# A convolution-and-attention kernel whose image seams are rebuilt: the next image's first convolution piece inside the last attention unit, spread statistics, and pools on exchanged sides

## The chip, the cores and the metric

The kernel runs on one core of one Trainium2 chip. The metric is the device time of one execution in microseconds (us), lower is better. All data are 32-bit floats, and the on-chip memory (SBUF) has 128 partitions, one per channel or token of a tile.

The engines are TensorE (PE, matmuls; PEld is its weight load), VectorE (DVE), ScalarE (ACT), GpSimd (POOL) and SyncE (SP). ACT, POOL and SP also issue transfers (DMAs), each from a queue of its own that is worked off in order.

## The reference, cut to what matters

The input holds 4 images of 128 channels and 64 x 64 positions (4096 tokens). Each image goes through three layers; what comes out has the input's shape.

```python
# layer 0: 1x1 convolutions of the group-normalised image, attention over all 4096 positions
x = x + _L0_conv_ref(_gn(x), w1, b1, a1, w2, b2, a2, wa, ba, aa)
#   e1, e2 = prelu(w1 x + b1), prelu(w2 x + b2)      (64 rows each)
#   out = softmax(e1^T e2) . prelu(wa x + ba)^T
# layer 1: "quantum ring" attention with 16 heads of 8, then a small feed-forward network
t = _to_tokens(x)
t = t + _L1_attn_ref(_ln_t(t), rx_theta, ry_theta, w_comb, ...)
#   q = ring(cos(heads + rx)); scores = q q^T / sqrt(8); ctx = softmax(scores) q
# layer 2: a linear map, normalised over all tokens of all images, and a recurrent scan
t = t + _L1_ffn_ref(_ln_t(t), W, V, gamma, beta)
x = _from_tokens(t, x)
```

The group norm `_gn` needs the mean and variance of every 4 channels over the whole image before the first convolution can begin.

## The kernel before, in words

The main loop handles the images one after another. For each one, `first_stage` (pools named `conv{n}`) does layer 0, and `second_stage` (pools named `attn{n}`) the 16-head attention of layer 1. The feed-forward network of image n is worked off in small steps between the matmuls of image n+1's first stage; that of image 3 has a `last_stage` of its own. Then comes the scan over all images.

**First stage.** `layer0` begins with `first_pieces`: two 512-column pieces of the image are normalised (L393), multiplied by the joined weights for queries and keys (`conv_matmuls`, L406), passed through two relus (L413, L414) and joined (`conv_joins`, L425 to L430) into `e12` and `e2`. The values come from `third_matmuls` (a bias matmul at L274, four at L442) and a prelu (L352 to L354). `halves` splits the first 512 queries into a high and a low part (L499, L500), two copies on ACT (L480) put them on the other 64 partitions, and then the softmax attention over 8 query groups `ic` and 16 key pairs `jp` can begin: scores (L518), exponentials (L522), weighing (L529). The other convolution pieces (`both_convs`, `third_conv`) are done between the first steps of that loop. `take` copies each result (`taken`, in the `half` pool), and `tokens` turns it to token order: `px` and `pt` are transposes on PE (L269), `sum` (L640) adds up the softmax sums held in `total` (pool `sums`). Its last parts write the layer 1 queries into `parts_dram`, from where the second stage reads them.

**Second stage.** `attention` runs over 8 head pairs and 4 query blocks each. A block has 20 units (blocks 0 and 1) or 16 units (blocks 2 and 3). Each unit has four score matmuls (L1072), the exponentials (ACT, L1084), transposes of them (VectorE, L847), mirrored products (PE, L860; added up by VectorE, L874) and weighing (PE, L881). `finish` ends a block: VectorE transposes the result into `o` (L919, a tile of the pool `half`, which has one buffer here), and POOL copies it out in 16 small copies (L927). `prepare` loads the queries (L777) and the keys (L786) of a pair from `parts_dram` through SP; of the four key blocks, block 1 is loaded first. Both pools have six buffers. While an image's attention goes on, its input `xs` is no longer wanted, and the function `exps` uses that memory as further buffers.

**The next image.** `prepare_image` is a generator that the attention calls in its last block: at unit 0 it loads the next image into `xs` (L142), and in the last eleven units it does the eight `bn_stats` (L365), the aggregate (L368), and the two small matmuls over the groups of four channels (L372, L381), with `rsqrt` (L217 on VectorE, L219 on POOL). For image 0 the same function runs before `layer0`, and between its steps the generator `first_weights` changes signs of `aa` and `a12` (L297, L298) and splits a bias row (L302, L303). The first eight weight loads come through ACT's queue (L150, L163, L173).

**Order and memory.** The order of PE, ACT and VectorE (in the attention of POOL too) is the one written in the code; SP's queue is put in order by the framework's scheduler. A stage's pools are stacked from the left or the right end of SBUF, in the order in which `stage` opens them. A buffer of a new pool may lie on memory of a closed one: its first writer waits until the old tile's last reader is done. Image n's `q` (16 KB per partition) lies at the left end for even and at the right end for odd n. Before, all pools of a first stage lie on the left (default), as do those of a second stage, but for the keys, which for even images lie on the right. Sizes per partition: a `HALF` tile has 2 KB, `MID` 4 KB, `BIG` 16 KB, a key tile 4 KB, a query tile 2 KB.

Of the kernel before, what the change touches and what calls it, by code (L numbers as in the profile page):

```python
# [26 lines left out]
def kernel(  # L27
# [31 lines left out]
    nc = tc.nc  # L59
# [28 lines left out]
    def stage(name, sides={}, others={}, **pools):  # L88
# [3 lines left out]
        with ExitStack() as stack:  # L92
            for kind, (shape, bufs) in pools.items():
                space = PSUM if kind.startswith("ps_") else bass.MemoryType.SB
                pool = stack.enter_context(
# [4 lines left out]
                        side=sides.get(kind),  # L100
# [4 lines left out]
            here.update(others)  # L105
            yield
# [39 lines left out]
    loader = [nc.scalar]  # L146
# [25 lines left out]
    for i, ap in enumerate((a1, a2)):  # L172
        nc.scalar.dma_start(out=a12_sb[ts(i, CR), :], in_=ap.partition_broadcast(CR))  # L173
# [187 lines left out]
    def norm_stats(n, xs):  # L361

        st = once.tile([P, NIC, 6], F32, tag="gst", name=f"gst{n}")
        for i in range(NIC):
            nc.vector.bn_stats(st[:, i, :], xs[:, ts(i, IC)])  # L365
            yield
# [5 lines left out]
        nc.tensor.matmul(pg[:, 0:1], grp, mv[:, 0:1], **alone)  # L372
        gm = once.tile([P, 1], F32, tag="gm", name=f"gm{n}")
# [7 lines left out]
        nc.tensor.matmul(pv[:, 0:1], grp, tv, **alone)  # L381
        yield gm, rsqrt(pv[:, 0:1], 1e-5, [P, 1], f"g{n}")

    def layer0(n, xs, xh, norm, shifted, begin, meanwhile):
# [13 lines left out]
        asmT = big_tile(f"asmT{n}")  # L398

# [17 lines left out]
        def conv_joins(i, j0, j1, y, z):  # L417

            cols = slice((2 * i + j0) * IC, (2 * i + j1) * IC)

            def parted(ap):
                return ap.rearrange("p (a b) -> p a b", b=IC)

            joined = parted(e12[:, cols])
            nc.vector.scalar_tensor_tensor(  # L425
                joined, z[:, j0:j1], a12_sb, y[:, j0:j1], ALU.mult, ALU.add
            )
            high, low = parted(e2[CR:P, cols]), parted(e2[0:CR, cols])
            nc.vector.tensor_copy(high.bitcast(F32R), joined[CR:P])
            nc.vector.tensor_tensor(low.bitcast(F32R), joined[CR:P], high, ALU.subtract)  # L430
# [7 lines left out]
        def third_matmuls(i, j, to):  # L438

            bias_first(to, 0)  # L440
            for k in range(TG):
                nc.tensor.matmul(  # L442
                    to[:, ts(k, P)],
                    xh[:, ts(TG * (2 * i + j) + k, P)],
                    wa_sb,
                    start=False,
                    stop=True,
                    skip_group_check=True,
                )

        def third_conv(i):
# [4 lines left out]
            to = pair(asmT[:, ts(i, 2 * IC)])  # L456
# [5 lines left out]
        def first_pieces():  # L462

            normalised(0, 1)
            pc = pair_psum(f"pc{n}_0")
            conv_matmuls(0, (0,), pc)
            normalised(1, 2)
            conv_matmuls(0, (1,), pc)
            early = conv_relus(0, 0, 1, pc)
            pas = [one_psum(f"pa{n}_0_{j}") for j in range(2)]  # L470
            for j in range(2):
                third_matmuls(0, j, pas[j])
            conv_joins(0, 0, 1, *early)
            if not shifted:
                halves(0)
            late = conv_relus(0, 1, 2, pc)
            if not shifted:
                for y in range(2):
                    hl = state["halves", 0][:, y, :].bitcast(F32R)
                    nc.scalar.copy(hl[CR:P], hl[0:CR])  # L480

            def join_third(j):
                ya, za = half_tile(f"ya{n}_0_{j}"), half_tile(f"za{n}_0_{j}")
                prelu(asmT[:, ts(j, IC)], pas[j], ya, za, (0.0, 0.0), aa_sb)
# [1554 lines left out]
```

## Time and profile before

| what | value |
|---|---|
| time, median of 3 runs | 6962.41 us (6960.99 to 6967.05) |
| the profiled execution's own time | 6967.16 us |
| its span in the profile | 6965.4 us |
| mean clock granted to TensorE | 0.988 |
| ACT L1084, exponentials of the 16 heads, two targets | 2953.1 + 1840.6 us |
| VectorE L847, their transposes, two sources | 2594.3 + 1562.5 us |
| PE L860 / L881 / L1072, second stage | 1969.8 / 1525.6 + 942.3 / 1245.7 us |
| PE L529 / L518, first stage | 947.1 / 588.6 us |
| ACT L522, exponentials of the first stage | 500.1 us |
| POOL L927, copies of `o` | 430.4 us |

The groups in the page's list give a line of the code, an engine, an operation, the tiles written and read, and the total busy time. The profile covers one execution; its span begins a little after the start of the time that is measured and ends a little before its end. Durations of single instructions are taken from this execution. DMAs of 256 KB each make up the keys (256 of them) and, among others, the loads of the images from `x`; the queries are 1024 DMAs of 32 KB, all from SP's queue. SP stands waiting for L1072 before its L786 loads for 1425.7 us in 105 cases (the longest 29.0 us), and before its L777 loads for 1696.0 us in 52 cases (the longest 38.2 us).

### The profile page before, as it was taken

How to read it: one execution, taken by the hardware profiler on the slowest of the kernel's cores; microseconds unless marked ns; L12 is line 12 of the kernel's file. 1: busy time of each engine (PE TensorE's matmuls, PEld its weight loads, DVE VectorE, ACT ScalarE, POOL GpSimd, SP SyncE). 2: the span in 40 equal slices, each digit the busy share in tenths (PEclk: the TensorE clock that was granted, in tenths of full speed). 3: DMA queues.
4: the chain of work that ended last, by engine and by line, in shares of the span. 5: the costliest groups of instructions: out<-in, count | busy, mean ns of one | idle time of the engine just before them, and what ended most of it. 6: DMA issues, size and time to landing. Idle time of an engine off the chain costs nothing. (4 is left out here: it accounts for less than half of the span.)

```text
span 6965.4 us, 223500 instructions
## 1 busy us (share of the span) xinstructions
PE 6819.4 (98%) x92343; PEld 3661.7 (53%) x92343; DVE 5971.6 (86%) x8073; ACT 5936.1 (85%) x11841; POOL 2789.8 (40%) x10000
## 2 busy tenths in 40 slices
PE   9999999999999999999999999999999999999997
PEld 5545555555664555555565455555456555555555
DVE  6688889887888898888787889898978898889888
ACT  4479999996669999999665999999956699999985
POOL 0134444434333444443433344344343343444443
PEclk9999999999999999999999999999999999999998
DMA  1110000000111000000011100000001100000012
GB/s 32 40 37 25 25 27 21 22 10 23 46 52 42 28 21 22 21 22 9 31 49 52 37 22 21 21 21 24 22 22 50 50 33 21 22 24 24 20 62 110
DMA packets 85975, 219.86 MB, mean 32 GB/s; under 512 B 10008, under 2 KB 11040, under 8 KB 84176
## 3 DMA queue, kind: packets, MB, share of 16 engines
q1 hardware_dynamic: 82316, 200.09, 8.5%
q8 instruction: 726, 11.89, 0.7%
q10 hardware_dynamic: 2628, 5.38, 0.2%
q14 instruction: 305, 2.50, 0.1%
HBM read 141.44 MB, written 56.62 MB: 28 GB/s over the span
## 5 line engine op out<-in xcount | busy, mean ns | idle before, releaser
L1084 ACT ACTIVATE e<-s 128x1024 f32<-128x1024 f32 (+1 forms) x3480 | 2953.1, 903 | 115.4 <-PE s L1072 84.6
L847 DVE STREAM_TRANSPOSE t<-e 128x1024 f32<-128x1024 f32 x2240 | 2594.3, 1210 | 78.0 <-ACT e L1084 75.3
L860 PEld LDWEIGHTS misc<-t,mirror 128*32 128x32 f32 x57344 | 1657.0, 110 | 1327.2 <-issue 1272.7
L860 PE MATMUL misc<-t,mirror 128*32 128x128 f32 x57344 | 1969.8, 273 | 16.8 <-DVE later L874 14.0
L1084 ACT ACTIVATE xs<-s 128x1024 f32<-128x1024 f32 (+1 forms) x2152 | 1840.6, 909 | 52.7 <-PE s L1072 40.8
L847 DVE STREAM_TRANSPOSE t<-xs 128x1024 f32<-128x1024 f32 x1344 | 1562.5, 1210 | 42.7 <-ACT xs L1084 41.3
L881 PE MATMUL acc<-e,q_aug 128*32 128x512 f32 x11360 | 1525.6, 609 | 0.0
L1072 PE MATMUL s<-queries,keys 32*128 32x512 f32 x9216 | 1245.7, 497 | 20.7 <-ACT e L1084 9.3
L927 POOL COPY own<-o 32x36 f32<-32x36 f32 x2048 | 430.4, 210 | 1803.1 <-DVE o L919 1723.2
L529 PE MATMUL acc<-p,asmT 128*128 128x512 f32 x2048 | 947.1, 594 | 0.4 <-ACT p L522 0.4
L881 PE MATMUL acc<-xs,q_aug 128*32 128x512 f32 x7072 | 942.3, 605 | 0.0
L522 ACT ACTIVATE p<-s 128x1024 f32<-128x1024 f32 x512 | 500.1, 1023 | 402.9 <-PE s L518 398.9
L1072 PEld LDWEIGHTS s<-queries,keys 32*128 32x128 f32 x9216 | 488.1, 182 | 602.3 <-issue 299.8
L952 POOL COPY other<-turned 32x64 f32<-32x64 f32 x1904 | 451.9, 237 | 622.5 <-DVE turned L942 544.0
L1084 ACT ACTIVATION_READ_ACCUMULATOR e<-s 128x1 f32 x2880 | 695.6, 242 | 0.0
L817 POOL COPY mirror<-q 32x128 f32<-32x128 f32 x2048 | 604.1, 295 | 198.6 <-PE misc L860 110.7
L518 PE MATMUL s<-hl,e 128*128 128x512 f32 x2048 | 588.6, 428 | 22.7 <-ACT hl L480 11.3
L543 DVE TENSOR_TENSOR total<-total,p 128x1024 f32<-128x1024 f32 x448 | 547.7, 1223 | 24.7 <-ACT p L522 17.3
L529 PEld LDWEIGHTS acc<-p,asmT 128*128 128x128 f32 x2048 | 380.1, 190 | 334.0 <-issue 310.4
L518 PEld LDWEIGHTS s<-hl,e 128*128 128x128 f32 x2048 | 380.7, 189 | 180.2 <-issue 69.2
L1084 ACT ACTIVATION_READ_ACCUMULATOR xs<-s 128x1 f32 x1728 | 421.7, 244 | 0.0
L913 POOL COPY by_token<-by_key 32x4 f32<-32x4 f32 x2000 | 385.5, 193 | 84.5
(320 smaller groups left out, 4440.3 us busy)
## 6 DMA issues: line engine op xcount, KB each, us to landing
keys<-parts_dram SPq DMA_DIRECT2D x256, 256.0 KB
queries<-parts_dram SPq DMA_DIRECT2D x1024, 32.0 KB
x_dram<-x SPq DMA_DIRECT2D x56, 256.0 KB
fx<-x_dram SPq DMA_DIRECT2D x48, 256.0 KB
t_dram<-t2T SPq DMA_DIRECT2D x32, 256.0 KB
t2s<-t_dram SPq DMA_DIRECT2D x16, 512.0 KB
hl<-hl SPq DMA_DIRECT2D x28, 256.0 KB
parts_dram<-high SPq DMA_DIRECT2D x28, 256.0 KB
```

The costliest lines, as they stand in the source:

```text
L518: nc.tensor.matmul(s[:, j, :], stationary, moving, start=y == 0, stop=y == len(parts) - 1)
L522: nc.scalar.activation(p, s, AF.Exp)
L529: nc.tensor.matmul(state["acc", ic], asmT[:, ts(2 * jp + j, P)], p[:, j, :], start=jp == 0 and j == 0, stop=jp == NP - 1 and j == 1,)
L543: nc.vector.tensor_tensor(state[ic], state[ic], p, ALU.add)
L817: nc.gpsimd.tensor_copy(wv[ts(a, 32), s, :, :, ts(a, D)], own[ts(s, 32)])
L847: nc.vector.transpose(group["e"][h][:, k, :], es[h])
L860: nc.tensor.matmul(state["acc"][ts(2 * x + h, 32), :], state["w"][:, QT * (s // 4) + TG * x + s % 4, h, :], state["e"][h][:, :, ds(IC * x ...
L881: nc.tensor.matmul(it["in"]["acc"][ts(2 * h + x, 32), :], it["qa"][:, ds((2 * it["tiles"][x] + h) * V, 32)], it["e"][h][:, ts(x, IC)], sta ...
L927: nc.gpsimd.tensor_copy(own[ts(s, 32), ts(x, 4), h, :], ov[ts(2 * h + x, 32), s, :, 0:V])
L952: copy(to[ts(k, 32), h], tv[ts(2 * x + h, 32), k])
L1072: nc.tensor.matmul(ss[h][:, x, :], keys[unit[x] // QT].bitcast(F32R)[r, ts(unit[x] % QT, P)], queries[b].bitcast(F32R)[r, :], start=True, ...
L1084: nc.scalar.activation(es[h][:, ts(x, IC)] if split else es[h], ss[h][:, x, :] if split else ss[h].rearrange("p x c -> p (x c)"), AF.Exp, ...
```

## The change

The change has five parts.

1. **The first piece.** `first_pieces` is gone. A new generator `opening` does the first 512 columns only (normalise, the joined and the value convolution, joins, split, copies). For images 1 to 3 it is stepped by the attention in the last unit of its last block: a step after the exponentials, a step after the weighing, a step at the end of the unit, and the rest behind the loop. The second piece (`second_piece`) comes after the first scores of `layer0`, and the other normalises are spread over the loop.
2. **Where it lies.** `stage` can close some pools early. The attention's `queries` and `keys` are closed in the last unit, and `place_of_first` puts the query halves `hl` and three tiles (the first 512 columns of keys, values and joined) into their memory; `rooms`, a pool for scratch, follows. `e12`, `e2` and `asmT` of `layer0` are 512 columns shorter, and `beyond` picks the tile of a column.
3. **Statistics.** For images 1 to 3 the eight pieces of the next image are loaded a second time, each into a tile of the pool `half`, and `bn_stats` is done on that tile: the load at unit 5, the `bn_stats` at unit 9 of blocks 2 and 3 of each pair, from the first pair on.
4. **Pools.** The first stage's pools all lie on the side away from the image's `q`, in a new order (`mid`, `e`, `big`, `sums`, `thalf`, `half`, then `x1`, `fhalf`, `hT`). Keys and queries of the second stage lie on the image's own side, its other pools on the other side, with `fixed` further ahead.
5. **The start.** The first eight weight loads go through POOL's queue instead of ACT's, and `first_weights` is stepped during `opening` instead of during the statistics of image 0.

```diff
-    def stage(name, sides={}, others={}, **pools):
+    def stage(name, sides={}, others={}, early=(), **pools):
...
+            soon = stack.enter_context(ExitStack())
...
-                pool = stack.enter_context(
+                pool = (soon if kind in early else stack).enter_context(
...
+            here["early"] = soon.close
...
-    loader = [nc.scalar]
+    loader = [nc.gpsimd]
...
-        nc.scalar.dma_start(out=a12_sb[ts(i, CR), :], in_=ap.partition_broadcast(CR))
+        nc.gpsimd.dma_start(out=a12_sb[ts(i, CR), :], in_=ap.partition_broadcast(CR))
...
-    def norm_stats(n, xs):
+    def norm_stats(n, xs=None):
...
-            nc.vector.bn_stats(st[:, i, :], xs[:, ts(i, IC)])
+            part = ts(i, IC)
+            if xs is None:
+                src = half_tile(f"early{n}_{i}")
+                nc.sync.dma_start(out=src, in_=x_rows[ts(n, P), part])
+                yield
+            else:
+                src = xs[:, part]
+            nc.vector.bn_stats(st[:, i, :], src)
...
+    def place_of_first(n, side):
+
+        stack = ExitStack()
+        hl = stack.enter_context(tc.tile_pool(name=f"hl{n}", bufs=2, side=side, reuse_waits="tile"))
+        pool = stack.enter_context(
+            tc.tile_pool(name=f"first{n}", bufs=1, side=side, reuse_waits="tile")
+        )
+        tiles = {
+            name: pool.tile([P, IC], F32, tag=name, name=f"first_{name}{n}")
+            for name in ("e2", "asmT", "e12")
+        }
+        return {"pool": (hl, list(MID)), "close": stack.close, **tiles}
+
+    def opening(n, xs, norm, opened, room, psum):
+
+        gm, rstd = norm
+        xh = room(f"xh{n}_0")
+        nc.vector.tensor_scalar(xh, xs[:, 0:IC], gm, rstd, ALU.subtract, ALU.mult)
+        yield
+        pc = psum(f"pc{n}_0")
+        nc.tensor.matmul(pc[:, 0, :], w12_sb, xh, start=True, stop=True)
+        third_into(pc[:, 1, :], lambda k: xh[:, ts(k, P)])
+        yield
+        y, z = room(f"y{n}_0_0"), room(f"z{n}_0_0")
+        nc.scalar.activation(y, pc[:, 0, :], AF.Relu, bias=b12_sb)
+        nc.scalar.activation(z, pc[:, 0, :], AF.Relu, bias=minus_b12, scale=-1.0)
+        joins(opened["e12"], opened["e2"], y.unsqueeze(1), z.unsqueeze(1))
+        opened["hl"] = hl = opened["pool"][0].tile(list(MID), F32, tag="hl", name=f"hl{n}_0")
+        split(hl, opened["e12"][0:CR])
+        yield
+        ya, za = room(f"ya{n}_0_0"), room(f"za{n}_0_0")
+        prelu(opened["asmT"], pc[:, 1, :], ya, za, (0.0, 0.0), aa_sb)
+        for y in range(2):
+            part = hl[:, y, :].bitcast(F32R)
+            nc.scalar.copy(part[CR:P], part[0:CR])
...
+        def second_piece():
+
+            pc = pair_psum(f"pc{n}_0_1")
             conv_matmuls(0, (1,), pc)
+            third_matmuls(0, 1, pc[:, 0, :])
+            y, z = conv_relus(0, 1, 2, pc)
+            conv_joins(0, 1, 2, y, z)
+            ya, za = half_tile(f"ya{n}_0_1"), half_tile(f"za{n}_0_1")
+            prelu(asmT[:, 0:IC], pc[:, 0, :], ya, za, (0.0, 0.0), aa_sb)
             normalised(2, 4)
...
-        joins = first_pieces()
-        pieces = [lambda: (joins(), both_convs(1)), lambda: third_conv(1)]
-        for i in range(2, NIC // 2):
+        normalised(1, 2)
+        pieces = [second_piece]
+        for i in range(1, NIC // 2):
             pieces += [lambda i=i: both_convs(i), lambda i=i: third_conv(i)]
...
                 if ic == jp == 0:
                     before, fresh = fresh, []
+                    if pieces:
+                        pieces.pop(0)()
+                if ic == 0 and jp in (2, 4) and not shifted:
+                    normalised(jp + 2, jp + 4)
...
+                    closing = end_of_all and at == len(tiles) - 1
+                    if closing:
+                        next(upcoming[1], None)
...
                         weigh(it)
                         if it["last"]:
                             finish(*it["block"])
+                    if closing:
+                        next(upcoming[1], None)
                     credit -= run_pending(turn, int(credit))
...
-                    if end_of_all and (at == 0 or at >= len(tiles) - NIC - 3):
-                        next(upcoming, None)
+                    if end_of_all and at in (0, len(tiles) - 1):
+                        next(upcoming[1], None)
+                    if not end_of_all and b > 1 and at in (5, 9):
+                        next(upcoming[0], None)
...
-        held_late = dict(thalf=(HALF, 6), half=(HALF, 2), hl=(MID, 2))
-        rest = dict(e=(BIG, 2), big=(BIG, 1), mid=(MID, 7), sums=(MID, 2))
-        pools = {**ffn, **held_late, **rest}
+        held_late = dict(thalf=(HALF, 6), half=(HALF, 2))
+        less = (P, S - IC)
+        rest = dict(mid=(MID, 7), e=(less, 2), big=(less, 1), sums=(MID, 2))
+        pools = {**rest, **held_late, **ffn}
...
+        other_side = {"left": "right", "right": "left"}[im["side"]]
+        opened = im["opened"] or place_of_first(n, other_side)
...
+        with stage(f"conv{n}", {"all": other_side}, others, **pools, **psum), tc.manual_schedule(engines=engines):
...
-        sides = {"keys": "right"} if im["side"] == "left" else {}
+        other_side = {"left": "right", "right": "left"}[im["side"]]
+        sides = {"all": other_side, "keys": im["side"], "queries": im["side"]}
...
-        with stage(f"attn{n}", sides, others, **pools):
+        with stage(f"attn{n}", sides, others, ("queries", "keys"), **pools):
...
+            here["early"]()
+            x_next["opened"] = opened = place_of_first(n, side)
+            with tc.tile_pool(name=f"rooms{n}", bufs=1, side=side, reuse_waits="tile") as pool:
```

## The prediction, made before the changed kernel ran

> **What bounds the kernel now.** I read the page's busy shares first, then the chain that ended last, then the timelines of the places that the change touches.
>
> ```profile
> PE 6819.4 (98%) x92343; PEld 3661.7 (53%) x92343; DVE 5971.6 (86%) x8073; ACT 5936.1 (85%) x11841; POOL 2789.8 (40%) x10000
> ...
> PE 41%; DVE 3%; issue 0%; ACT 0%; POOL 0%; DMA 0%; SPq 0%; DVEq 0%; ACTq 0%; POOLq 0%
> ```
>
> TensorE is busy for 6819.4 of 6965.4 us, and the chain runs mostly through it. So the whole kernel has 146 us of PE idle time, and no edit here takes a matmul away for good: the change can only move, close or open holes in PE. The seams between images hold such holes. The PE timeline where image 0's attention ends and image 1's convolution begins (start, busy time, operation; in brackets the idle time before it and what ended it):
>
> ```profile
> 1632.37 0.50 PE L1072 MATMUL s<-queries,keys 32*128 32x512 f32 x2 [0.27 <-ACT e L1084]
> ...
> 1634.54 0.86 PE L860 MATMUL misc<-t,mirror 128*32 128x128 f32 x24 [0.68 <-DVE later L874]
> ...
> 1637.05 0.50 PE L1072 MATMUL s<-queries,keys 32*128 32x512 f32 x2 [1.22 <-ACT e L1084]
> ...
> 1646.24 0.38 PE L372 MATMUL misc<-gmv,grp 128*128 128x1 f32 x2 [1.97 <-DVE later L874]
> ...
> 1655.21 1.98 PE L406 MATMUL pc<-q,w_sb 128*128 128x512 f32 x4
> ...
> 1662.24 0.49 PE L518 MATMUL s<-hl,e 128*128 128x512 f32 x1 [2.80 <-ACT hl L480]
> 1662.90 2.80 PE L518 MATMUL s<-hl,e 128*128 128x512 f32 x7 [0.17 <-ACT hl L480]
> ```
>
> The reader is to see two groups of holes. Before the piece's first matmul (L406) they make 0.27+0.68+1.22+1.97 = 4.14 us; between its last matmul and the first scores (L518) 2.80+0.17. Why the first group: the table of busy time per stretch (stretch, length, then busy us and instructions of PE, PEld, DVE, ACT, POOL; the number before the last two is the granted clock).
>
> ```profile
> 1618.00:1646.00 28.00, 24.11 (x420) 12.18 (x412) 27.87 (x35) 23.03 (x53) 6.76 (x30) 1.00 0.11 42
> 1646.50:1649.90 3.40, 3.40 (x34) 1.57 (x37) 0.54 (x3) 1.94 (x2) 0.00 (x0) 0.50 0.02 5
> 1663.60:1666.90 3.30, 3.30 (x8) 2.04 (x7) 2.84 (x6) 2.54 (x4) 3.00 (x7) 0.50 0.00 0
> 3350.50:3353.90 3.40, 3.40 (x80) 2.35 (x79) 0.54 (x3) 1.94 (x2) 0.00 (x0) 1.00 0.00 0
> ```
>
> In the attention's last 28 us VectorE is full (27.87), and eight bn_stats (L365, 0.58 us apart) are in it. Right behind the holes the clock granted to PE is 0.50 for a stretch of 3.4 us, twice in this seam and twice in the third (5059.8, 5076.9), not in the second (last row).
>
> **B1, the statistics leave the attention's end.** Eight bn_stats, 8 × 0.58 = 4.6 us, and the aggregate (0.36) leave a VectorE that is full; the same 4.14 us of holes go. Three seams: −12.4. The bn_stats go one by one into blocks 2 and 3 of pairs 0 to 3. There PE is busy for 154.30 of 154.40 us and VectorE for 138.41 (the stretch of one pair, 2268.9 to 2423.3): 0.58 us per block is covered by VectorE's 16 idle us. Each needs a load of 256 KB through SP, into the buffer in which a block's `o` lies: in block 3 of pair 0 POOL has copied `o` out at 2393.95 (16 copies, 3.98 us), SP is idle between two loads there (2393.6 to 2405.6), and the bn_stats is due in unit 9, at about 2408: 14 us of cover. Behind the load in SP stand only keys that wait for PE anyway. Cost 0.
>
> **B2, the first piece goes into the last unit.** After the last unit's scores PE has weigh (0.87), the piece's own matmuls (0.5 for L406 and 1.55 for L274/L442: 2.05), then 64 mirror steps, 16 weighs and 64 mirror steps (1.86, 1.74, 1.86): 8.9 us with the scores. The piece's chain on the other engines is normalise 0.46, matmul 0.5, two relus 2 × 0.58, join 0.74, 0.42 and 0.69, split 0.42 and 0.68, two copies of 0.62: about 7.2 us from the scores on; the normalise, whose room lies on the keys' memory, waits for these scores with the unit's flips (L847) behind it on VectorE. It ends 1.7 us before PE runs out, so the first scores of the convolution wait for nothing: −2.97, and −0.19 behind it. But the second piece now comes right after these scores, and what follows it waits for its chain (pc, exps, relus, joins, normalise): I work out 1.85 us of new holes. Net −1.3 per seam, −3.9. The bounds: 0, where the last flips hold the chain back, and −3.2, where the second piece is hidden as well.
>
> **B3, the clock.** The same work takes 75.77 us in seam 1 and 73.08 in seam 2, holes alike: two stretches at half clock cost 2.69. Seams 1 and 3 give −5.4 at most, 0 at least; with holes of at most 1 us left I take −4.5. [...]
>
> **A, the start.** VectorE's timeline:
>
> ```profile
> 10.14 0.37 DVE L368 BATCH_NORM_AGGREGATE gmv<-gst 128x2 f32<-128x48 f32 x1
> 15.54 0.15 DVE L297 TENSOR_SCALAR a_sb<-a_sb 128x1 f32<-128x1 f32 x1 [5.03 <-DMA a_sb<-in_a_dram]
> ...
> 17.92 1.00 DVE L393 TENSOR_SCALAR q<-xs,gm,r_g 128x512 f32<-128x512 f32 x2 [0.69 <-POOL r_g L219]
> ```
>
> The sign steps (L297) wait 5.03 us for a1 and a2 with the mean's copy (L374) queued behind them. They move behind the normalise, which then begins at about 13.5 instead of 17.92. The gain is not 4.4: the join needs a1 and a2, and the second piece's 2.05 us of matmuls now follow the first scores. By my sum the second conv pair (L406 at 31.12) moves to 29.3: −1.8. The eight weight loads go from ACT's queue to POOL's; no DMA from POOL is in this trace. ACT issues them from 4.51 to 12.18, and the last lands at 15.5; POOL could begin at about 0.4, but its set-up (2.8 us of work that now ends at 3.2, the matrix `grp` for the mean at 10.65 in it) then stands behind eight issues; after it POOL is idle until 17.3. I bound the term by −4.4 (weights not late) and +5 (all as late again as the stall now seen), and take −1.8, nearest to the row. [...]
>
> **C, the pools change sides.** Attention 2 starts late (PE, then SP, then VectorE of attentions 1 and 2):
>
> ```profile
> 3804.32 0.43 PE L640 MATMUL sum<-total,ones 128*32 128x128 f32 x8
> 3804.67 0.66 PE L269 MATMUL pt<-ident,taken 128*128 128x128 f32 x4
> 3811.18 0.89 PE L1072 MATMUL s<-queries,keys 32*128 32x512 f32 x2 [5.85 <-DMA keys<-parts_dram]
> ...
> 3804.80 0.55 SPq L786 DMA_DIRECT2D keys<-parts_dram  x1
> ...
> 2157.74 0.72 DVE L919 STREAM_TRANSPOSE o<-acc 128x512 f32<-128x512 f32 x1 [0.85 <-PE acc L881]
> ...
> 3867.43 0.72 DVE L919 STREAM_TRANSPOSE o<-acc 128x512 f32<-128x512 f32 x1 [0.85 <-PE acc L881]
> ```
>
> The first keys are loaded only after the last sums (L640): their buffer lies on the convolution's `sums`. From the end of pt to the first finish (L919) it takes 62.10 us here (3867.43 − 3805.33), 53.70 in attention 1, 53.89 and 52.82 in 0 and 3: a loss of 8.4. Adding up the pools (KB per partition): before, keys of even images (right end, 24 KB) met a stack from the left of 16 for q and, at its end, `sums`, 152 KB in all; room ends under 176, as the overlap itself shows. After, on even images keys lie over x1, fhalf and hT, whose last use is 20 us earlier: −8.4. On odd images the stack from the left is the previous q 16, hl 8, first 6, mid 28, e 28, big 14, sums 8, thalf 12, half 4: 124 KB; from the right q, queries and keys take 16+12+24 = 52. The sum is 176 again, so the same inequality that shows in image 2 says that keys of images 1 and 3 lie over `half`, whose `taken` is read by pt, the last matmul before the attention. The stall appears there instead, 0.6 later: +9.0 and +9.9 (image 3 lacks 0.9 of the others' start). Net +10.5. If keys were loaded from the other end of their pool first, it would be −8.4.
>
> **D, the rest:** the piece's `e12`, `e2`, values in tiles of their own cost no instruction; two one-column matmuls move; the last stage's loads wait for other buffers. +1, between 0 and +3.
>
> **Sum:** −12.4 −3.9 −4.5 −1.8 +10.5 +1 = −11.1. The profiled execution took 6967.16 (span 6965.4 and 1.76 around it), 4.75 over the median of the runs, 6962.41. Against the median: **6951.3**.
>
> **Rivals.** (1) *No stall in images 1 and 3*: the room or the order within the pool spares the first-loaded keys. Then C is −8.4 instead of +10.5: −30, **6932**. For it: a few hundred bytes decide; against: the sums agree to the KB with a case that the trace shows. Chance 0.22. (2) *Slower: the early loads of x get stuck in SP's queue.* SP stands at L786 up to 29.0 us and at L777 up to 38.2 for PE. If in block 3 a load is put behind the next pair's keys, it leaves after 2418.3 instead of 2394 and lands some 10 us after the bn_stats is due at 2408; all flips queue behind that on VectorE, PE has two units (4 us) of cover: 6 us, 12 blocks, +72, and −11 beside it: +61, 7023; stuck behind the first keys only (2405.6), 12 × 2 = +24: **6975 to 7023**. It decides from unit 11 of the block on. For it: SP's order is not written by hand; against: SP is free from 2393.6 to 2405.6. Chance 0.12. (3) *It doesn't do what it says*: the new piece waits behind the flips of the last unit, so PE stands as long as now; B2 0, B3 0, B1 halved: −6.2 −1.8 +11.5 = +3.5, **6966**. Against: 1.7 us of slack. Chance 0.12. The forecast keeps 0.54.
>
> **Range and chances.** A measurement of this kernel tells about 0.2%, 13.9 us, from no change: faster is below 6948.5, slower above 6976.3. The forecast's own range is 6942 to 6960 (B3 and A from end to end, less likely at once). The range takes in the first and third rival: **6925 to 6969**. Faster: all of rival 1 and two fifths of the forecast, 0.22 + 0.22 = 0.44. Slower: rival 2, 0.12, and 0.01 of rival 3: 0.13. The rest 0.43.
>
> **What would show it.** In the changed trace: no hole in front of the statistics' matmul, bn_stats spread over four pairs, a pair still at 154.4 us; the first L518 of images 1 to 3 without a wait on hl; clock 1.00 at the seams; the mean's copy near 11 us; keys' DMA wait gone in attention 2, and one of 6 us in attentions 1 and 3. The last is what most likely breaks the forecast; a DMA wait in front of a bn_stats is the next.

## The result, and the profile after

The changed kernel takes 6992.3 us (median of 6 runs, 6987.85 to 6994.54), the kernel before 6963.86 us beside it on the same chip: a ratio of 1.004, interval 1.0027 to 1.0053. Slower by 28 us, where 6951.3 was forecast and the range ended at 6969. The profiled executions differ by 27.4 us (spans 6992.8 and 6965.4). The page of the changed kernel, the two rows that answer to those of before:

```profile
PE 6821.0 (98%) x92343; PEld 3662.4 (52%) x92343; DVE 5975.2 (85%) x8073; ACT 5935.2 (85%) x11841; POOL 2790.9 (40%) x10008
...
PE 89%; DVE 8%; issue 1%; ACT 1%; DMA 1%; POOL 0%; SPq 0%; DVEq 0%; ACTq 0%; POOLq 0%
```

Every engine does the work that it did before (PE 1.6 us more of 6819). So the 27 us are holes (PE stands for 171.8 us instead of 146.0), and the page doesn't say where. (Its row of the chain can't be compared with that of before: there the chain is followed over 44% of the span only, 41% on PE, so "the chain runs mostly through it" in the prediction was read from less than half of the execution.) To find the place I laid fixed marks over both traces: the end of each VectorE transpose into `o`, which closes a block ("finish", numbered 0 to 31 within an attention), and the end of each copy `taken` on ACT, which closes a query group of the first stage ("take" 0 to 7). The stretches between them, in us, the first two kernels and the ones told of below (seam: from finish 22, past the attention's end, to take 0 of the next image; attention start: from take 7 to finish 0):

| stretch | before | after | x_store | x_half | x_early | b_spread | b_e_last | x_best |
|---|---|---|---|---|---|---|---|---|
| start to take 0, image 0 | 86.85 | 92.28 | 92.27 | 92.01 | 86.37 | 86.80 | 86.68 | 87.26 |
| take 0 to take 7, image 0 | 312.46 | 311.46 | 311.45 | 311.44 | 311.46 | 311.28 | 312.50 | 309.76 |
| attention start, image 0 | 55.36 | 55.11 | 55.12 | 57.99 | 55.23 | 54.09 | 55.86 | 54.24 |
| attention start, image 1 | 55.18 | 63.92 | 63.47 | 55.48 | 63.52 | 55.36 | 56.98 | 55.39 |
| attention start, image 2 | 63.58 | 62.89 | 54.61 | 54.21 | 61.64 | 63.86 | 55.33 | 54.35 |
| attention start, image 3 | 54.30 | 63.52 | 62.78 | 55.19 | 63.77 | 55.13 | 55.86 | 54.84 |
| finish 18 to 22, image 0 | 154.36 | 156.18 | 156.17 | 156.17 | 156.17 | 156.11 | 156.16 | 156.07 |
| seam 1 | 421.92 | 420.05 | 419.93 | 419.05 | 413.20 | 415.85 | 413.60 | 412.98 |
| seam 2 | 419.26 | 420.04 | 420.88 | 419.88 | 413.44 | 413.73 | 415.66 | 412.84 |
| seam 3 | 421.92 | 420.94 | 419.10 | 420.02 | 414.80 | 413.62 | 413.68 | 412.86 |
| span | 6965.36 | 6992.80 | 6981.63 | 6966.40 | 6964.58 | 6950.13 | 6946.68 | 6934.59 |

Against before, the changed kernel loses 4.4 us in image 0's first stage (+5.43 and −1.00), 17.3 at the attention starts (−0.25 in image 0 left out: +8.74 −0.69 +9.22), 5.8 between finish 18 and 22 of three attentions (+1.82 in the one shown), and wins only 2.1 in three seams (−1.87 +0.78 −0.98). That is 25.4 of the 27.4 us; 1.3 of the rest lie in the early pairs, where the spread bn_stats are.

**The seam.** PE's timeline at the place shown of before:

```profile
1649.35 1.12 PE L442 MATMUL pc<-xh_room,w_sb 128*128 128x512 f32 x2
...
1656.87 2.11 PE L566 MATMUL s<-hl,first_e 128*128 128x512 f32 x8
1662.82 1.17 PE L495 MATMUL pc<-q,w_sb 128*128 128x512 f32 x2 [3.84 <-DVE q L467]
...
1670.96 3.44 PE L495 MATMUL pc<-q,w_sb 128*128 128x512 f32 x4 [2.56 <-DVE q L467]
```

The first piece (L442) is done inside the last unit, and the first scores (L566) wait for nothing: both old holes are gone. Right behind them stand two new ones of 3.84 and 2.56 us, both in front of the second and third convolution pieces, both for a normalise (L467) on VectorE. VectorE's timeline tells why:

```profile
1661.47 0.77 DVE L996 STREAM_TRANSPOSE room<-later 128x256 f32<-128x256 f32 x2 [3.18 <-POOL own L981]
1662.16 0.51 DVE L467 TENSOR_SCALAR q<-xs,gm,r_g 128x512 f32<-128x512 f32 x1
...
1670.28 1.00 DVE L467 TENSOR_SCALAR q<-xs,gm,r_g 128x512 f32<-128x512 f32 x2
```

The second piece's normalise is behind two transposes of the attention's end (L996), and these wait 3.18 us for POOL to copy `o` out of the buffer that they write (16 copies, 1657.45 to 1661.43). Before, both normalises (L393) stood ahead of them, and the wait for the same copies was there already, 2.03 us:

```profile
1652.55 1.00 DVE L393 TENSOR_SCALAR q<-xs,gm,r_g 128x512 f32<-128x512 f32 x2 [0.67 <-POOL r_g L219]
...
1658.46 0.77 DVE L942 STREAM_TRANSPOSE room<-later 128x256 f32<-128x256 f32 x2 [2.03 <-POOL own L927]
```

In the kernel before it held up the first piece's joins, which follow it on VectorE; now it holds up the second piece. In the changed kernel the next normalise (1670.28) stands behind the second piece's joins and prelu. The granted clock (number before the last two) is 0.50 in stretches behind the holes; these now exist in seam 2 as well, which had none:

```profile
1663.70:1667.10 3.40, 3.40 (x12) 2.70 (x11) 0.00 (x0) 0.94 (x2) 2.83 (x15) 0.50 0.00 0
...
3377.20:3380.60 3.40, 3.40 (x12) 2.70 (x11) 0.00 (x0) 0.98 (x2) 2.83 (x15) 0.50 0.00 0
```

**The attention starts.** SP's timeline in images 1 and 2, then PE's:

```profile
2108.81 0.61 SPq L840 DMA_DIRECT2D keys<-parts_dram  x1
2110.09 0.32 SPq L716 DMA_DIRECT2D x_dram<-xs  x1
2110.46 3.08 SPq L840 DMA_DIRECT2D keys<-parts_dram  x5
...
3804.17 0.60 SPq L840 DMA_DIRECT2D keys<-parts_dram  x1
3823.71 0.33 SPq L716 DMA_DIRECT2D x_dram<-xs  x1
3824.09 3.12 SPq L840 DMA_DIRECT2D keys<-parts_dram  x5
```

```profile
2108.09 0.66 PE L271 MATMUL pt<-ident,taken 128*128 128x128 f32 x4
2114.84 0.89 PE L1126 MATMUL s<-queries,keys 32*128 32x512 f32 x2 [6.09 <-issue]
...
3831.16 1.31 PE L1126 MATMUL s<-queries,keys 32*128 32x512 f32 x6 [8.37 <-issue]
```

In image 1 the first key load leaves right after pt (2108.09 to 2108.75): the memory wait that was forecast, with the 9 us that were forecast. In image 2 the first load leaves 18 us before the end of pt, so its memory is free as forecast, and PE still stands for 8.37 us: the five other loads are behind the store of the last x0 (L716), which waits for VectorE until 3823.71. SP holds the same order in both images: one key load, the store, five key loads. In the kernel before it had this order in image 2 already, with little to wait for at the store:

```profile
3806.67 0.32 SPq L662 DMA_DIRECT2D x_dram<-xs  x1
3807.05 2.83 SPq L786 DMA_DIRECT2D keys<-parts_dram  x5
```

**The start.** PE's timeline of image 0:

```profile
23.41 4.08 PE L566 MATMUL s<-hl,first_e 128*128 128x512 f32 x8 [4.41 <-ACT hl L456]
...
34.79 3.00 PE L495 MATMUL pc<-q,w_sb 128*128 128x512 f32 x4 [2.92 <-DVE q L467]
```

The first scores come at 23.41 instead of 26.50, and the second conv pair (L495) at 34.79 instead of 31.12: the same normalise behind the second piece's joins as in the seams. Up to 39 us the clock is at half for 17.1 us (11.66 to 18.48, 21.90 to 28.72, 35.55 to 38.96), before for 10.2 (11.51 to 21.75).

### The profile page after: what moved, and what is told of

Same layout as the page of the kernel before. It is cut to its first block, busy times and chain, and to the rows that moved or that the text cites. A ratio compares the mean times of both kernels' runs of the same rounds, so it can differ in the third digit from the quotient of the medians.

```text
span 6992.8 us, 223555 instructions
## 1 busy us (share of the span) xinstructions
PE 6821.0 (98%) x92343; PEld 3662.4 (52%) x92343; DVE 5975.2 (85%) x8073; ACT 5935.2 (85%) x11841; POOL 2790.9 (40%) x10008
## 4 chain that ended last, share of the span: by engine, by line
PE 89%; DVE 8%; issue 1%; ACT 1%; DMA 1%; POOL 0%; SPq 0%; DVEq 0%; ACTq 0%; POOLq 0%
PE acc L935 31%; PE misc L914 21%; PE s L1126 14%; PE acc L577 11%; PE s L566 6%; DVE t L901 3%; PE pf L1337 1%; PE pc L495 0%; DVE t2s L1956 0%; DVE total L591 0%; PE pt L271 0%; PE pwx L1562 0%; PE pw L1263 0%; PE pa L418 0%; PE ph L1316 0%
## 5 line engine op out<-in xcount | busy, mean ns | idle before, releaser
L1126 PE MATMUL s<-queries,keys 32*128 32x512 f32 x9216 | 1246.0, 497 | 31.4 <-issue 20.5
L577 PE MATMUL acc<-p,asmT 128*128 128x512 f32 x1792 | 825.2, 593 | 0.0
L566 PE MATMUL s<-hl,e 128*128 128x512 f32 x1792 | 513.4, 428 | 11.5 <-ACT p L570 10.8
L577 PEld LDWEIGHTS acc<-p,asmT 128*128 128x128 f32 x1792 | 333.1, 190 | 296.6 <-issue 277.0
L566 PEld LDWEIGHTS s<-hl,e 128*128 128x128 f32 x1792 | 331.8, 188 | 150.2 <-issue 66.1
```

Source lines behind the costliest of these rows:

```text
L566: nc.tensor.matmul(s[:, j, :], stationary, moving, start=y == 0, stop=y == len(parts) - 1)
L577: nc.tensor.matmul(state["acc", ic], values_at(tile_of(2 * jp + j)), p[:, j, :], start=jp == 0 and j == 0, stop=jp == NP - 1 and j == 1,)
L1126: nc.tensor.matmul(ss[h][:, x, :], keys[unit[x] // QT].bitcast(F32R)[r, ts(unit[x] % QT, P)], queries[b].bitcast(F32R)[r, :], start=True, ...
```

## The experiments

Times are medians; the kernel before took 6961.85 beside the first four, 6962.90 beside the next four and 6960.33 beside the last two.

### x_store: the store of the last x0 behind the first keys

```diff
-        if not biased:
+        if not biased and not last:
             nc.sync.dma_start(out=im["x0"][:, cols], in_=x0)
         yield last
+        if last:
+            nc.sync.dma_start(out=im["x0"][:, cols], in_=x0)
```

> The changed kernel with one line moved: the store of the last token group's x0 is issued one step later, after the first keys. Theory (order in SP's queue, memory second): in image 2 the first key block's second half waits in SP behind that store (SP stands from 3804.83 to 3823.71), so from the end of pt to the first finish it takes about 54 us instead of 62; in images 1 and 3 the first half still waits for pt by its memory, and only the 1.3 us between the two halves go (about 61.4 left). Together some -11 us against the changed kernel. Rival (the memory holds the keys in all three images): nothing moves, 62.1 to 62.7 in all three.

6983.36 us, ratio to before 1.0032 (1.002 to 1.0043). Image 2's attention start falls from 62.89 to 54.61, those of images 1 and 3 by 0.45 and 0.74 (1.3 expected). SP's timeline of this kernel:

```profile
2108.64 3.55 SPq L842 DMA_DIRECT2D keys<-parts_dram  x6
...
3804.63 20.40 SPq L842 DMA_DIRECT2D keys<-parts_dram  x6
3825.15 0.41 SPq L719 DMA_DIRECT2D x_dram<-xs  x1
```

The store now follows all six key loads, and in image 2 that ends the stall. But the row of 20.40 us hides a wait: two loads, the two halves of the key block that is loaded first, leave at 3804.63 and 3805.29; the other four come from 3822.89 on, after pt. SP's waits of the whole kernel (total, times, longest) name pt as what they waited for, 18.3 us at most:

```profile
SPq L842 <- PE pt L271: 53.5, 3, 18.3
```

So of the five loads behind the store only one, the second half of the first block, could have left earlier. That one was what PE stood for: with it ahead of the store PE waits 0.95 us instead of 8.37. In image 1 the loads still begin only after pt.

### x_half: the pool `half` opened first

```diff
-        pools = {**rest, **held_late, **ffn}
+        pools = {"half": held_late["half"], **rest, "thalf": held_late["thalf"], **ffn}
```

> The changed kernel with the convolution's pool half opened first instead of seventh, so that the keys of images 1 and 3 lie over thalf, whose last use is some 20 us before the attention. Theory (memory under the first keys holds images 1 and 3, and the place in SP's queue follows from it): from pt to the first finish about 54 us in images 1, 2 and 3, -26 us in all against the changed kernel. Rival A (SP's order alone, whatever the memory): 62 us stay in all three. Rival B (memory alone, image 2 has another cause): 54 us in 1 and 3, 62 in image 2, -17 us.

6967.34 us, 1.0009 (0.9999 to 1.0019). All three stalls go: −8.44, −8.68, −8.33. SP's timeline in image 1:

```profile
2092.10 3.59 SPq L840 DMA_DIRECT2D keys<-parts_dram  x6
2111.58 0.32 SPq L716 DMA_DIRECT2D x_dram<-xs  x1
```

The keys leave 17 us earlier and ahead of the store, which was not moved in the code. So both rivals fall: what lies under the keys decides the stall in images 1 and 3, and with it the scheduler's place for the store changes in all three, image 2 included. In image 2 all six leave early here (its attention start takes 54.21 us), so with this order of the pools the memory of the four that waited in x_store is free too. Why the scheduler had put the second half of the first block behind the store in the changed kernel, though its memory was free, is not shown. A price that I had not foreseen: image 0's attention start is 2.9 us longer, with PE waiting 2.11 us for POOL's copy of `q_aug`.

### x_early: the normalises ahead

```diff
-            for name in ("e2", "asmT", "e12")
+            for name in ("e2", "asmT", "e12", "xh1")
...
         nc.vector.tensor_scalar(xh, xs[:, 0:IC], gm, rstd, ALU.subtract, ALU.mult)
+        nc.vector.tensor_scalar(opened["xh1"], xs[:, ts(1, IC)], gm, rstd, ALU.subtract, ALU.mult)
...
-            conv_matmuls(0, (1,), pc)
-            third_matmuls(0, 1, pc[:, 0, :])
+            xh1 = opened["xh1"]
+            nc.tensor.matmul(pc[:, 1, :], w12_sb, xh1, start=True, stop=True)
+            third_into(pc[:, 0, :], lambda k: xh1[:, ts(k, P)])
...
-            normalised(2, 4)
...
-        normalised(1, 2)
+        normalised(2, 4)
```

> The changed kernel with the second piece normalised right behind the first, into a tile of its own, and the third and fourth normalised before the second piece's joins. Theory (the second piece's chain on VectorE is what is late: its normalise stands behind two transposes that wait for POOL's copies of o, 3.84 us of PE, and the next normalise behind the joins, 2.56 us): both holes fall to some 0.5 us in each of three seams, the one of 2.92 us at the start too, and the stretches at half clock behind them shrink; -6 to -9 us per seam and -3 to -6 at the start, -20 to -32 in all. Rival (ACT's relus and exponentials or the two PSUM buffers hold the second piece): the holes stay within 2 us of what they are under another name, -6 us in all.

6966.82 us, 1.0006 (0.9997 to 1.0016). The seams are 6.85, 6.60 and 6.14 us shorter than in the changed kernel, the start 5.91: −25.5 in all. PE's timeline in seam 1:

```profile
1651.04 2.14 PE L567 MATMUL s<-hl,first_e 128*128 128x512 f32 x8
1653.43 1.13 PE L536 MATMUL pc<-first_xh,w_sb 128*128 128x512 f32 x2 [0.25 <-ACT p L571]
...
1657.23 1.88 PE L496 MATMUL pc<-q,w_sb 128*128 128x512 f32 x4
```

Of 6.40 us of holes 0.25 are left at this place, and seams 1 and 2 have no stretch at half clock. The theory holds: two normalises in the wrong place on VectorE. But some 55 us further on a hole of 2.3 us is new in each seam (see x_best), and seam 3 (414.80 us, the other two 413.20 and 413.44) has a stretch at half clock behind it.

### b_spread: the statistics alone

The kernel before with the changed `norm_stats` (its steps and the load of the next image are now two lists, `upcoming[0]` and `upcoming[1]`), and

```diff
-                    if end_of_all and (at == 0 or at >= len(tiles) - NIC - 3):
-                        next(upcoming, None)
+                    if end_of_all and at == 0:
+                        next(upcoming[1], None)
+                    if not end_of_all and b > 1 and at in (5, 9):
+                        next(upcoming[0], None)
```

> The kernel before with the spread statistics alone: the pieces of x loaded early, bn_stats in blocks 2 and 3 from the first pair on, nothing of the statistics in the last block. Theory (each seam's end gains what the changed kernel shows between the finishes around it, about 3 us on the mean, and pays 1.24 and 0.52 us in pairs 4 and 5, where the mirrored products on PE wait for VectorE's reading of the two small results): -1.2 to -2.4 us per image, -4 to -7 in all. Rival (as predicted: 4.14 us per seam go and nothing is paid): -12.4 us. Rival (the loads get stuck in SP's queue): bn_stats wait for DMA, slower by over 20 us.

6951.70 us, 0.9983 (0.9974 to 0.9993): 10 us faster. My theory was too low, and the prediction's own −12.4 nearer, though something is paid. The seams win 6.07, 5.53 and 8.30, and finish 18 to 22 costs 1.75 to 1.84 in each of the three images that have a next one. PE's timeline in seam 1:

```profile
1634.00 0.50 PE L1083 MATMUL s<-queries,keys 32*128 32x512 f32 x2 [0.19 <-ACT e L1095]
...
1654.81 4.02 PE L529 MATMUL s<-hl,e 128*128 128x512 f32 x8 [2.81 <-ACT hl L491]
```

Of the 4.14 us in front of the first piece 0.19 are left; the hole of 2.8 in front of the first scores stays, as it must. None of the spread bn_stats waits for a DMA, here or in the changed kernel (0 of 24 there).

### x_scalar: the weights back on ACT's queue

```diff
-    loader = [nc.gpsimd]
+    loader = [nc.scalar]
...
-        nc.gpsimd.dma_start(out=a12_sb[ts(i, CR), :], in_=ap.partition_broadcast(CR))
+        nc.scalar.dma_start(out=a12_sb[ts(i, CR), :], in_=ap.partition_broadcast(CR))
```

> The changed kernel with the first eight weight loads back on ACT's queue. Theory (on POOL's queue they are issued from 1.3 to 5.9 us, beside the pieces of x, and on ACT's from 4.5 to 12.2, behind them; so x lands later: the aggregate ends at 11.7 instead of 10.5): the aggregate is 1.1 us earlier, the first take of image 0 (92.3) about 1 us earlier, nothing else moves. Rival (the loads' place in the queue decides the whole loss of 5.4 us at the start): the first take falls to some 87 us. Rival (weights on ACT's queue are late for the join): it rises.

6990.39 us, 1.0041 (1.0026 to 1.0057). The aggregate ends at 10.40 us instead of 11.66, the first take at 91.48 instead of 92.28. So in the changed kernel the queue costs 0.8 us of the 5.4 at the start, and the misplaced normalise more than the rest: x_early, which leaves the queue alone, brings the first take to 86.37. With the normalises mended the queue's 0.8 us don't come on top: x_best has both edits and 87.26, with PE waiting 0.72 us for a bias row (L276 for L305).

### b_best and b_late: two that miss

b_best is b_spread with `thalf` opened last:

```diff
-        pools = {**ffn, **held_late, **rest}
+        thalf = held_late.pop("thalf")
+        pools = {**ffn, **held_late, **rest, "thalf": thalf}
```

> The kernel before with the spread statistics and with thalf opened last, so that image 2's first keys lie over thalf instead of sums; the first piece stays where it was before. Theory (spread statistics are what is gained in the seam, the piece inside the attention adds little to them): -8.5 us against the spread statistics alone, about 6943, within 4 us of the corrected change. Rival (the piece inside the attention is worth the 2.8 us hole in front of the first scores in each seam): the corrected change is 8 us or more ahead of this.

6961.73 us, 1.0 (0.999 to 1.0009), some 19 us above the expectation. Image 2's attention start is repaired (55.40), but the stretch from finish 31 to the next take is 88.08 in seam 2 instead of 70.06. VectorE's timeline there:

```profile
3359.24 0.43 DVE L510 CAST hl<-e 64x512 fp32r<-64x512 f32 x1 [8.12 <-POOL own L965]
```

Moving `thalf` moved `half` and `hl` by 12 KB, and they now lie on the rooms of the attention's end, which POOL is still reading: hl waits 8.12 us, and `ya` on ACT another 8.13 for the same copies.

b_late adds to it:

```diff
-                    if not end_of_all and b > 1 and at in (5, 9):
+                    if b > 1 and at in ((5, 9) if pair < 4 else (4, 6, 8, 10, 12) if end_of_all else ()):
```

> As the one before with one more step: bn_stats stay spread over pairs 0 to 3, but the aggregate and the two small matmuls go back into the attention's last block. Theory (the 1.24 and 0.52 us in pairs 4 and 5 are the two matmuls, 0.7 us, and two short waits that they cause on PE, 1.0 us): from finish 18 to 22 of an attention 154.4 us instead of 156.2, and the last block longer by 0.7; -1 us per image. Rival (the aggregate is what hurt the last block too): the last block is longer by 2 us or more, and nothing is won.

6980.77 us, 1.0027 (1.0015 to 1.0038): 19 us worse than b_best. Finish 18 to 22 is back at 154.32, but from finish 22 to 31 it takes 352.47 instead of 343.45. PE's timeline:

```profile
1631.61 1.04 PE L871 MATMUL misc<-t,mirror 128*32 128x128 f32 x24 [2.27 <-DVE gm L383]
...
1645.62 1.81 PE L871 MATMUL misc<-t,mirror 128*32 128x128 f32 x32 [2.55 <-DVE v_g L217]
```

The rival was right: at these places (units 4 to 12, where the kernel before had its bn_stats; it did the aggregate and the small matmuls at the very end of the block) the two readings of the small results on VectorE are more than the last block can bear: it takes longer without the bn_stats than the kernel before with all of the statistics (350.79). In the changed kernel the same wait in pair 4 is much smaller:

```profile
1166.08 1.52 PE L914 MATMUL misc<-t,mirror 128*32 128x128 f32 x48 [0.72 <-DVE gm L385]
```

### x_best, b_e_last: what the first piece is worth

x_best is the changed kernel with the edits of x_early and x_scalar, and `half` and `thalf` exchanged:

```diff
-        pools = {**rest, **held_late, **ffn}
+        pools = {**rest, "half": held_late["half"], "thalf": held_late["thalf"], **ffn}
```

> The changed kernel with three corrections: the pools half and thalf exchanged, the second piece's and the next two normalises early, the weights back on ACT's queue. Theory (the losses add up): -26 us at the attentions' starts, -20 in three seams, -6 to -7 at the start, so some 52 us less than the changed kernel, about 6940; and no start of image 0's attention that is 2.9 us longer, as with half opened first. Rival (holes closed at the seams come back as waits for POOL or DMA): the gain is under 40 us.

6940.66 us, 0.997 (0.9958 to 0.9982): 51.6 us below the changed kernel, and faster than both kernels of this study. The losses add up, and image 0's attention start (54.24) is spared. But the rival was right in kind: each seam has a new hole, which neither the changed kernel nor the kernel before has there. ACT's row and PE's in seam 1:

```profile
1706.18 1.65 ACT L263 ACTIVATE fx<-fx,less_v,r_v 128x128 f32<-128x128 f32 x4 [7.12 <-POOL less_v L256]
...
1708.78 2.12 PE L567 MATMUL s<-hl,first_e 128*128 128x512 f32 x8 [2.08 <-ACT p L571]
```

The exponentials that PE waits for stand on ACT behind a step of the feed-forward (L263), and this waits for POOL, which works off the copies and sums of the attention's end until 1704.57. In b_spread and in the changed kernel ACT waits 3.35 us at that step and PE not at all; with the seam earlier on the other engines it is 7.1 to 7.3 us and a hole of 2.1 to 2.3 in each seam. That is read from the rows; no run moves POOL's copies.

b_e_last is b_spread with the keys of image 2 over another pool:

```diff
-        pools = {**ffn, **held_late, **rest}
+        e = rest.pop("e")
+        pools = {**ffn, **held_late, **rest, "e": e}
```

> The kernel before with the spread statistics, and with the pool e opened last, so that image 2's first keys lie over e2 (last read by the last scores, 9 us before pt) instead of sums; thalf, half and hl stay where they were. Theory (the 18 us that the order with thalf last lost between images 1 and 2 came from hl and ya lying on the attention's last rooms, which POOL still copied): this seam is at 70 us again, image 2's start at 55, in all some 8.5 us below the spread statistics alone, about 6943. Rival (the loss came from the keys' new place): the seam stays at 88 us.

> The corrected change once more, beside the kernel above on the same chip: about 6940. Theory (the first piece inside the attention adds little once the statistics are spread): the two are within 4 us. Rival (it is worth the hole of 2.8 us in each of three seams): this one is 8 us or more ahead.

b_e_last takes 6950.12 us, 0.9984 (0.9975 to 0.9993), x_best again 6941.11, 0.9973 (0.9963 to 0.9983). Image 2's start is 55.33 and seam 2 from finish 31 is 72.03: the theory on hl and ya holds, its rival falls. But of the 8.5 us that image 2's start won, 1.6 remain in the medians, and nothing against the kernel before, which took 1.5 us less beside it. In the traces image 0's stretch from take 0 to take 7 and the other three attention starts are 0.7 to 1.8 us longer than in b_spread, without one wait that stands out. The seams differ by the clock: a stretch of 6.8 us at half lies in seam 1 in b_spread (1654.36 to 1661.18) and in seam 2 in b_e_last (3356.48 to 3363.31), with the same hole of 2.81 us in every seam, and the seam that has it is 2.2 and 1.9 us longer than its like.

And x_best is 9 us ahead where I expected at most 4, which is the rival's number, but not for the rival's reason. Where no clock is lost, a seam takes 412.84 to 413.29 us in x_best (five seams of its two traces) and 413.61 to 413.73 in b_spread and b_e_last (four): the first piece is worth 0.3 to 0.9 us per seam, not 2.8. The hole of 2.8 in front of the first scores is gone, and the new one of 2.1 to 2.3 behind POOL's copies has come for it. Of the 12.1 us between the two profiled executions (spans 6934.59 and 6946.68) 4.3 lie in the seams, about 2 of these in the clock of b_e_last's seam 2; 5.2 lie in the four attention starts and 2.2 in image 0's first stage (between its takes the clock is at half for 6.8 us in b_e_last and never in x_best). Why these last two differ stays open.

## Why the prediction was wrong

The forecast was −11.1, measured are +27.4 in the profiled executions. By the stretches, of the 38.5 us between them some 26 lie in B1 to B3 (the seams, finish 18 to 22 and the early pairs make +5.0 in place of −20.8), 7 in C and 6 in A. Point by point:

- **B2 is the step that failed most.** The part up to the first scores came true: they wait for nothing, and the 2.97 us are gone. That was close: the chain took 8.8 us from the scores on (1647.91 to the end of the copies at 1656.69), not 7.2, since the relus wait for the value matmuls as well (ACT 1.18 us for L418), and of the 1.7 us of slack some 0.2 were there. The step "I work out 1.85 us of new holes" for the second piece measured 3.84 + 2.56 = 6.40 us, with two stretches at half clock behind them. I had costed the piece's own chain and not what stands ahead of it on VectorE: the last transposes, behind POOL's copies of `o`, a wait that the trace of before shows at 1658.46. x_early moves two normalises and wins 6.1 to 6.9 us per seam. Even so the first piece is worth 0.3 to 0.9 us per seam at full clock (x_best), not 1.3: what POOL still has to copy comes back as a hole of 2.1 to 2.3 us.
- **B3** (−4.5) did not come, since holes were there again; of the two stretches of seam 1 one had stood in front of the first scores, now both stand behind them, and seam 2 has two as well. In x_best no such stretch lies in the three seams, in its second trace one does, in seam 3 (5104.36 to 5107.77, behind a hole of 2.27 us); in b_spread and in b_e_last, with one hole of 2.8 us in each seam, there is one, in seam 1 and in seam 2. So with holes of this size left it is not settled which seam pays. Nor do the sizes of the holes tell it: in seam 2 of before holes of 1.96 and 2.80 us, like those of seams 1 and 3 (1.97 and 2.80), brought no stretch, and stretches at half clock came with holes of 1.97 us (before, at 1646.5) and 2.81 us (b_spread, 1654.36 to 1661.18).
- **B1** was right in place: b_spread alone turns 4.14 us of holes into 0.19 and wins 10 us. Its size was not: the three seams win 19.9 us where 12.4 were forecast (the clock's part is in them: 13.7 us at half clock in the seams before, 6.8 in b_spread), and "Cost 0" was wrong: the spread bn_stats take 0.3 to 0.5 us per image up to finish 18, and what follows them in pairs 4 and 5 takes 1.8, 5.4 in all: the two small matmuls and PE's waits for VectorE's readings (0.72 and 0.30). B1 to B3 together were −20.8; with the normalises mended (x_best) the three seams and the price in pairs 4 and 5 give −24.4 + 5.1 = −19.3. That the sums meet is luck: the statistics give more than was forecast, the first piece less, and the price of 5.1 was put at nothing.
- **C** was right for images 1 and 3, in cause and size (+8.74, +9.22, forecast +9.0 and +9.9). "On even images keys lie over x1, fhalf and hT, whose last use is 20 us earlier: −8.4" failed: the memory of the block that PE needs first was free, but the queue was not (its second half stood behind the store), and the other blocks' memory was free only after pt (x_store, 3822.89). The trace of before had shown the pattern, a store of x0 between the first key load and the others (3806.67), and I read only the first load's wait.
- **A** (−1.8) measured +4.4. VectorE's wait for a1 and a2 did go, and the first scores came 3.1 us earlier. The sentence that the second conv pair "moves to 29.3" failed, it came at 34.79, by the same misplaced normalise; x_early wins back 5.9 us. The weights' queue, where I had feared +5, costs 0.8 in the changed kernel.
- **The rivals.** None of the three was it. The first (no stall in images 1 and 3) is excluded by the SP and PE rows, the second (early loads of x stuck in SP's queue) by the spread bn_stats, which wait for no DMA. The third had PE standing as long as before because the piece waits behind the last unit's flips; the piece doesn't wait, PE stands longer, behind it. The slow side came from a mechanism that I had in the text as a small term.

## What to carry to other kernels

When a piece of work is moved ahead, follow the next piece in the order of every engine: here it inherited the place, and what stood between the two (POOL's copies and the last transposes) then stood in front of it, 3.84 us of PE. And when that is mended, look for the engine that has the most left to do (here POOL, for which ACT then waited 7.1 to 7.3 us in x_best): its wait came next. Where pools of successive stages share memory, ask for each first tile of the new stage who reads its old tile last, and also where a scheduler will put its load among the other transfers of the queue; in image 2 of the changed kernel a free buffer did not help the load behind a store that waited until 3823.71, and PE stood for 8.37 us. And of a change with five parts the parts are worth measuring one by one: here one alone gave 10 us, and the others hid it.

## What the runs showed that I had not expected

The stalls at the attention's starts of images 1 and 3 cost more than their holes. Around them the clock is at half for longer: 23.9 us around image 1's in the changed kernel (2110.85 to 2127.92 and 2144.99 to 2151.81), 13.7 us in the kernel before, where there is no stall; around image 3's 20.5 against 10.2. PE's idle time there grew by 7.6 and 7.1 us, the stretches by 8.7 and 9.2. It is not the same each time: around image 2's start, stalled in both kernels, it was 23.9 us before and 17.1 after. The order in SP's queue changed with the place of a pool: opening `half` first sent six key loads (at 2092.10 in image 1) ahead of a store (2111.58) that no edit had touched.
